# Moving the second projection piece of an element from step 2 to step 3 in a two-layer attention kernel

## The chip, the cores and the metric

The kernel runs on one core of a Trainium2 chip. The metric is device time in microseconds (us): the median of three runs before the change is 3305.34 us (3304.78 to 3305.59). Everything is computed in fp32, and the whole batch is one launch.

## What is computed

The input is `x` of shape (8, 512, 32, 32): 8 batch elements, 512 channels, 1024 positions. Two layers follow each other. Cut to what matters:

```python
# layer 0: group norm, 8-head attention (64 channels a head), projection, group norm, residual
hn  = group_norm(x, gn1_scale, gn1_bias)
qkv = einsum('bchw,oc->bohw', hn, w_qkv) + b_qkv
wgt = softmax(einsum('bct,bcs->bts', q * scale, k * scale))      # per head, 1024 x 1024
a   = einsum('bts,bcs->bct', wgt, v)
x   = x + group_norm(einsum('bchw,oc->bohw', a, w_proj) + b_proj, gn2_scale, gn2_bias)
# layer 1: weight-normed projections, one 512-channel head, output projection, residual
qkv = einsum('oc,bcn->bon', weight_norm(v_qkv), x);  qkv = qkv / rms(qkv)
h   = einsum('bij,bcj->bci', softmax(q.T @ k * C**-0.5), v)
out = (x + einsum('oc,bcn->bon', weight_norm(v_out), h)) * 2**-0.5
```

## The kernel before, in words

A loop (`for b in range(B)`, L1015) goes over the 8 elements. In each, layer 0's attention runs as 32 **steps** (`STEPS`, L335; the loop of L1018): step i handles one block of 128 query positions of one pair of heads, with 8 blocks to a pair (`j, r = divmod(i, NB)`, L1019). After the steps come the last values, the output projection and norm of layer 0, and all of layer 1, except that most of layer 1's last products are carried into the first steps of the next element: `fills` and `laters` (L1124 and L1125) put `one.products(1, c)` and `one.keep(1, c)`, for c of 1, 2 and 3, into steps 0, 1 and 2 of element b + 1. Step 3 gets empty lists.

Nothing is reordered by a scheduler: `InOrder` (L26) pins the instructions of every engine to the order in which the program states them. So the order of the work around the change is that of `Heads.step` (L490):

- `softmax(i)` (L432): for each of two heads a VectorE maximum over the 128x1024 scores in PSUM, then a ScalarE exp from PSUM into the tile `p`, with its row sums.
- `values`, on steps 5, 7, 9 and so on: the attention values of two earlier steps, 32 matmul instructions into a bank `po`.
- `fill`: what the caller hands in for TensorE. Here that is, in this order, a carried product of layer 1 and one **piece** of projections.
- `scores(i + 1)` (L417): four matmul calls (eight instructions in the profile) into two tiles `s` of 128x1024. These tiles come from `ps_s`, which has three buffers (L101). The order of the calls is first half of head 0, first half of head 1, second halves.
- `turn()` (L444): VectorE transposes the `p` of the step before, and four DMAs on SP's queue write it to `pT`.
- `scale()` (L462): a VectorE reciprocal, then two GpSimd (POOL) multiplications on `p`.
- `later`: a carried `keep` (two VectorE operations and, for the second half of the positions, an output DMA on SP's queue), then the piece's GpSimd addition, then, on steps 1, 3, 5 and 7 of elements 1 to 6, one GpSimd group-norm application `norm1.apply` (L1037).

A **piece** is one `yield` of `project_rows` (L363). For the next pair of heads it makes half of k or half of q. Eight matmul calls (16 instructions) use only 64 of the 128 rows each and alternate between two banks of `ps_m`; that pool has two buffers in all (L102), which the carried products and the values use too. ScalarE then empties both banks (L394 and L395), one into `qk` and one into a spare part of the tile `v`, and a GpSimd addition (L396) sums them. The four pieces of pair j + 1 must be done when step 8j + 7 issues the first scores of that pair. One piece is taken from `todo` on each step on which `(i - LAG) % RG` is not 0. With `LAG` 5 and `RG` 2 these are the even steps; the odd ones from 5 on have values.

For elements 1 to 7 TensorE's order at the start is therefore:

```
step 0: po(c=1)  piece 0  s(1)
step 1: po(c=2)           s(2)
step 2: po(c=3)  piece 1  s(3)
step 3:                   s(4)
step 4:          piece 2  s(5)
step 5: values            s(6)
step 6:          piece 3  s(7)
```

Here po(c) is the carried product of layer 1 (eight calls, 16 instructions), and s(n) the scores of step n. The scores of step 0 are issued ahead of the loop. In element 0 there is no carried product; steps 0 to 3 have one part each of that element's own values projection (L1012).

Of the kernel before, what the change touches and what calls it, by code (L numbers as in the profile page):

```python
# [52 lines left out]
def attention_blocks_kernel(  # L53
# [52 lines left out]
    def big(name, lead=CI):  # L106

        return slots.take([P, lead, CI * N // lead], name)
# [41 lines left out]
    def load_x(b, xt, ci):  # L150
        SY.dma_start(out=xt[:, ci, :], in_=xv[b, :, ci, :])
# [181 lines left out]
    RG, TG = 2, 2 * P  # L333
    NB = N // P
    STEPS, LAG = CI * NB, 5  # L335
    halves = (slice(0, D), slice(D, P))

    def project_qk(b, j, hn):

        qk = pair.tile([P, 2, N], F32, tag="qk", name=f"qk_{b}_{j}")  # L340
        kp = qk[:, 1, :].rearrange("p (be m) -> p be m", be=4)

        def pieces():
            for t in (1, 0):
                w = near["qk"][:, t]
                for th in range(2):
                    hs = slice(th * HN, (th + 1) * HN)
                    pm = bank(f"pqk_{b}_{j}_{t}_{th}")
                    run(matmuls(pm, [(w[:, ci, j * P : (j + 1) * P], hn[:, ci, hs]) for ci in range(CI)]))
                    if t == 0:  # L350
                        AC.activation(qk[:, 0, hs], pm, AF.Identity, bias=bqs[:, j : j + 1], scale=QSCALE0)
                    else:
                        AC.activation(
                            kp[:, :, th * P : (th + 1) * P],
                            pm.rearrange("p (m be) -> p be m", be=4),
                            AF.Identity,
                            bias=col(BK, j),
                        )
                    yield

        return qk, pieces()

    def project_rows(b, j, hn):  # L363

        qk = pair.tile([P, 2, N], F32, tag="qk", name=f"qk_{b}_{j}")
        kp = qk[:, 1, :].rearrange("p (be m) -> p be m", be=4)
        spare = near["v#"]

        def pieces():
            for t in (1, 0):
                w = near["qk"][:, t]
                scale = 1.0 if t else QSCALE0
                bias = col(BK, j) if t else bqs[:, j : j + 1]
                for th in range(2):
                    hs = slice(th * HN, (th + 1) * HN)
                    pms = [bank(f"pqk_{b}_{j}_{t}_{th}_{r}") for r in range(2)]
                    for ci in range(CI):
                        for r in range(2):  # L380
                            PE.matmul(
                                pms[r],
                                w[halves[r], ci, j * P : (j + 1) * P],
                                hn[halves[r], ci, hs],
                                start=(ci == 0),
                                stop=(ci == CI - 1),
                            )
                    to, rest = qk[:, 0, hs], spare[:, hs]
                    if t:

                        to = kp[:, :, th * P : (th + 1) * P]
                        rest = rest.rearrange("p (be m) -> p be m", be=4)
                        pms = [pm.rearrange("p (m be) -> p be m", be=4) for pm in pms]
                    AC.activation(to, pms[0], AF.Identity, bias=bias, scale=scale)  # L394
                    AC.activation(rest, pms[1], AF.Copy, scale=scale)  # L395
                    yield lambda to=to, rest=rest: PO.tensor_add(to, to, rest)  # L396

        return qk, pieces()
# [112 lines left out]
    def project_out_half(b, h, o):  # L511

        for j in range(CI):
            for th in range(2):
                pm = bank(f"ph_{b}_{j}_{th}")
                run(matmuls(pm, out_terms(h.a, j, th, range(CI // 2))))
                AC.activation(o[:, j, th * HN : (th + 1) * HN], pm, AF.Identity, bias=col(BP, j))
            yield
# [482 lines left out]
    qk0, todo = project_qk(0, 0, x0)  # L1001
# [13 lines left out]
    for b in range(B):  # L1015
        hn, more = heads.hn, b + 1 < B
        todo = iter(())
        for i in range(STEPS):  # L1018
            j, r = divmod(i, NB)  # L1019
            due = []  # L1020
            fill = [lambda: due.append(next(todo, None))] if (i - LAG) % RG else []
            early, later = [], []
            if i < CI:
                fill, later = fills[i] + fill, laters[i]
            if r == 0:
                if j + 1 < CI:
                    heads.qk[j + 1], todo = project_rows(b, j + 1, hn)
                elif more:
                    qk_next, todo = project_rows(b + 1, 0, hn_next)
                if j + 1 == CI:  # L1030
                    slots.give(f"hn_{b}")
                    if not more:
                        o_last = big(f"o_{b}")
                        todo = project_out_half(b, heads, o_last)
            later.append(lambda: [f() for f in due if f])

            if b and more and i % 2 and i < 2 * CI:  # L1037
                later.append(lambda: norm1.apply(i // 2, PO))
            if not b:


                if i == CI:
                    hn_next = big(f"hn_{b + 1}")
                    norm1 = Norm1(b + 1, hn_next)
                if 0 <= i - CI < CI:
                    later.append(lambda: load_x(b + 1, hn_next, i - CI))
                if 0 <= i - CI - 2 < 2 * CI:
                    later.append(lambda: norm1.stats((i - CI - 2) // 2, i % 2))
                k = i - 3 * CI - 2
                if k == 0:  # L1050
                    coeffs = norm1.gn.all_steps()
                    early += [norm1.aggregate, lambda: next(coeffs)]
                elif 0 < k < 8:
                    early.append(lambda: next(coeffs, None))
                if 0 <= k - 7 < CI // 2:
                    for ci in range(2):
                        later.append(lambda ci=ci: norm1.apply(2 * (k - 7) + ci, PO))

            if i == STEPS - NB + 1:
                xt = big(f"x_{b}")  # L1060
            if 0 <= i - (STEPS - NB + 1) < CI:
                later.append(lambda: load_x(b, xt, i - (STEPS - NB + 1)))
            heads.step(i, fill, early, later)
# [105 lines left out]
```

## Time and profile before

The profiled execution took 3305.39 us, of which its span is 3303.4 us and 1.99 us lie around it. It stands 0.05 us above the median of the runs.

| what | value |
|---|---|
| median of 3 runs | 3305.34 us |
| profiled execution, and its span | 3305.39 us, 3303.4 us |
| granted TensorE clock, mean | 0.998 |
| VectorE (DVE) busy | 2123.7 us, 64% |
| ScalarE (ACT) busy | 1073.0 us, 32% |
| GpSimd (POOL) busy | 982.8 us, 30% |
| DMA, mean | 124 GB/s |

All instructions carry the line of the pinning helper, L34, so groups are told apart by their tiles: `s` scores, `pqk` projection pieces, `po` values or carried products, `nm` the maxima, `p` the probabilities. In the chain of waits, each row is a start, a length and what ran; a TensorE row there runs from the start of its first instruction to the start of what follows. In the timeline a matmul's length is longer, as its modelled end is shown and matmuls overlap.

### The profile page before, as it was taken

How to read it: one execution, taken by the hardware profiler on the slowest of the kernel's cores; microseconds unless marked ns; L12 is line 12 of the kernel's file. 1: busy time of each engine (PE TensorE's matmuls, PEld its weight loads, DVE VectorE, ACT ScalarE, POOL GpSimd, SP SyncE). 2: the span in 40 equal slices, each digit the busy share in tenths (PEclk: the TensorE clock that was granted, in tenths of full speed). 3: DMA queues.
4: the chain of work that ended last, by engine and by line, in shares of the span. 5: the costliest groups of instructions: out<-in, count | busy, mean ns of one | idle time of the engine just before them, and what ended most of it. 6: DMA issues, size and time to landing. Idle time of an engine off the chain costs nothing.

```text
span 3303.4 us, 35653 instructions
## 1 busy us (share of the span) xinstructions
PE 3261.8 (99%) x13178; PEld 1603.1 (49%) x13178; DVE 2123.7 (64%) x2869; ACT 1073.0 (32%) x1813; POOL 982.8 (30%) x857
## 2 busy tenths in 40 slices
PE   8999999999999999999999999999999999999899
PEld 4444544445444454444544445444454445444354
DVE  4696647855478655885458754686646866468653
ACT  2453114521145211551215412254122531235210
POOL 0352124511255012550215403253023531235111
PEclk9999999999999999999999999999999999999999
DMA  5575205741168411782127811277213762057600
GB/s 188 187 201 166 79 34 149 203 152 67 38 167 213 134 45 51 184 223 95 45 77 190 231 55 59 84 197 213 77 39 103 198 181 89 13 133 199 185 7 26
DMA packets 182708, 410.82 MB, mean 124 GB/s; under 512 B 27621, under 2 KB 27657, under 8 KB 176521
## 3 DMA queue, kind: packets, MB, share of 16 engines
q1 hardware_dynamic: 182416, 408.53, 43.7%
q8 instruction: 105, 1.72, 0.2%
q14 instruction: 67, 0.54, 0.0%
q10 hardware_dynamic: 120, 0.02, 0.0%
HBM read 112.48 MB, written 27.56 MB: 42 GB/s over the span
## 4 chain that ended last, share of the span: by engine, by line
PE 98%; DVE 1%; DMA 0%; issue 0%; ACT 0%; SPq 0%; ACTq 0%; DVEq 0%
PE po L34 27%; PE s L34 14%; PE pqk L34 14%; PE pv L34 7%; PE p_e_T L34 7%; PE p_e_B L34 5%; PE py L34 4%; PE p_u_T L34 3%; PE p_v_T L34 3%; PE p_o_T L34 3%; PE p_v_B L34 3%; PE p_u_B L34 2%; PE p_o_B L34 2%; PE pG L34 1%; PE pA L34 0%; PE pB L34 0%
## 5 line engine op out<-in xcount | busy, mean ns | idle before, releaser
L34 POOL TENSOR_SCALAR p<-p,tt 128x1024 f32<-128x1024 f32 x512 | 566.0, 1118 | 926.7 <-DVE tt L34 926.7
L34 ACT ACTIVATE p<-s,nm 128x1024 f32<-128x1024 f32 x512 | 565.5, 1109 | 848.7 <-DVE nm L34 799.3
L34 DVE TENSOR_REDUCE nm<-s 128x1 f32<-128x1024 f32 x512 | 602.7, 1219 | 224.5 <-PE s L34 224.3
L34 DVE STREAM_TRANSPOSE pb<-p 128x2048 f32<-128x2048 f32 x256 | 589.6, 2303 | 24.7 <-POOL p L34 19.3
L34 PE MATMUL s<-qk 64*128 64x512 f32 x2048 | 515.0, 603 | 12.4 <-ACT p L34 12.4
L34 PE MATMUL pqk<-hn,qk 64*128 64x512 f32 (+1 forms) x2016 | 479.9, 591 | 0.0
L34 PE MATMUL po<-pT,v 128*64 128x256 f32 x4096 | 470.3, 382 | 3.4 <-DMA pT<-pb 3.2
L34 PE MATMUL po<-e,v 128*128 128x512 f32 x1024 | 451.7, 595 | 0.0
L34 PEld LDWEIGHTS po<-pT,v 128*64 128x64 f32 x4096 | 284.1, 137 | 226.8 <-ACT v L34 79.6
L34 PEld LDWEIGHTS pqk<-hn,qk 64*128 64x128 f32 (+1 forms) x2016 | 204.3, 187 | 252.2 <-issue 243.0
L34 PEld LDWEIGHTS s<-qk 64*128 64x128 f32 x2048 | 196.1, 186 | 252.8 <-issue 232.9
L34 PEld LDWEIGHTS po<-e,v 128*128 128x128 f32 x1024 | 191.9, 190 | 245.0 <-issue 236.4
L34 POOL TENSOR_TENSOR u<-u,xy 128x512 f32<-128x512 f32 x64 | 79.0, 1272 | 770.7 <-DMA xy<-far_rinv 671.4
L34 PE MATMUL pv<-v,hn 128*128 128x512 f32 x512 | 229.0, 598 | 0.0
L34 DVE TENSOR_TENSOR e<-e,p_e_T 128x512 f32<-128x512 f32 x160 | 107.0, 685 | 145.1 <-PE p_e_T L34 142.9
L34 POOL TENSOR_TENSOR qk<-qk,v 128x512 f32<-128x512 f32 x124 | 158.2, 1276 | 83.9 <-ACT v L34 83.9
L34 ACT ACTIVATE e<-e,shift,rinv 128x512 f32<-128x512 f32 x128 | 100.9, 812 | 247.7 <-DVE e L34 247.7
L34 POOL TENSOR_TENSOR esum<-esum,e 128x512 f32<-128x512 f32 x96 | 121.5, 1267 | 163.9 <-ACT e L34 161.4
L34 PEld LDWEIGHTS pv<-v,hn 128*128 128x128 f32 x512 | 94.6, 190 | 115.1 <-issue 114.8
L34 PE MATMUL p_e_T<-s,t 128*128 128x512 f32 x320 | 147.8, 592 | 0.0
L34 PE MATMUL py<-x,gram 128*128 128x512 f32 x320 | 141.5, 602 | 6.0 <-issue 6.0
L34 ACT COPY v<-pv 128x1024 f32<-128x1024 f32 x32 | 32.2, 1007 | 259.4 <-PE pv L34 243.7
(186 smaller groups left out, 3068.3 us busy)
## 6 DMA issues: line engine op xcount, KB each, us to landing
pT<-pb SPq DMA_DIRECT2D x1024, 256.0 KB, 4.2
hn<-in_x_dram SPq DMA_DIRECT2D x32, 512.0 KB, 5.4
x<-in_x_dram SPq DMA_DIRECT2D x32, 512.0 KB, 5.6
out_dram<-x SPq DMA_DIRECT2D x32, 512.0 KB, 2.6
score<-far_score SPq DMA_DIRECT2D x8, 1792.0 KB, 7.5
value<-far_value SPq DMA_DIRECT2D x8, 1792.0 KB, 7.0
qk<-far_qk SPq DMA_DIRECT2D x7, 2048.0 KB, 7.9
proj<-far_proj SPq DMA_DIRECT2D x7, 1792.0 KB, 10.4
```

The source lines that it names most:

```text
L34: return lambda *args, **kw: self._pin(call(*args, **kw))
```

## The change

For elements 1 to 7, step 2 no longer takes a piece and step 3 takes one. All other steps, and element 0, are as before. A piece that is taken brings along its matmuls, its two ScalarE evictions and, in `later`, its GpSimd addition. Pieces then fall on steps 0, 3, 4 and 6 of the first pair of heads.

```diff
         for i in range(STEPS):
             j, r = divmod(i, NB)
             due = []
-            fill = [lambda: due.append(next(todo, None))] if (i - LAG) % RG else []
+
+            projects = (i - LAG) % RG if not b or i not in (2, 3) else i == 3
+            fill = [lambda: due.append(next(todo, None))] if projects else []
             early, later = [], []
             if i < CI:
                 fill, later = fills[i] + fill, laters[i]
```

TensorE's order at the start of elements 1 to 7 becomes:

```
step 0: po(c=1)  piece 0  s(1)
step 1: po(c=2)           s(2)
step 2: po(c=3)           s(3)
step 3:          piece 1  s(4)
step 4:          piece 2  s(5)
step 5: values            s(6)
step 6:          piece 3  s(7)
```

## The prediction

> **What bounds the kernel now.** I read the page first, its busy times and its chain.
>
> ```profile
> PE 3261.8 (99%) x13178; PEld 1603.1 (49%) x13178; DVE 2123.7 (64%) x2869; ACT 1073.0 (32%) x1813; POOL 982.8 (30%) x857
> ...
> PE 98%; DVE 1%; DMA 0%; issue 0%; ACT 0%; SPq 0%; ACTq 0%; DVEq 0%
> ```
>
> TensorE (PE) is busy nearly throughout, and 98% of the chain that ended last is PE. So a microsecond counts only if it comes off PE's own line. DVE's 1% is the hint: there are a few places where PE waits for the softmax. The waits, for PE alone, say where:
>
> ```profile
> PE s L34 <- ACT p L34: 12.4, 7, 1.8
> PE py L34 <- issue: 6.0, 1, 6.0
> ```
>
> The largest wait, twice the next, falls 7 times, and there are 7 elements with a step 3 that has only scores. The 1.8 us is counted from a modelled matmul end, so I take the size from the chain around step 3 of element 1, which begins where po(c=3) of step 2 has been issued:
>
> ```profile
> 526.23 4.05 PE pqk L34 x15
> ...
> 530.71 0.89 PE s L34 x5
> 531.60 0.02 issue
> 531.62 1.24 DVE nm L34
> ...
> 532.94 1.21 ACT p L34 x2
> ...
> 534.20 1.55 PE s L34 x5
> ...
> 536.18 3.00 PE pqk L34 x14
> ...
> 539.61 1.72 PE s L34 x7
> ```
>
> Read it as: piece 1 and s(3) up to 531.60; then nothing new on PE until 534.20, as s(4)'s second matmul needs the buffer that holds head 0 of s(3), which is free only after its maximum (1.24 us) and exp (1.21 us) have read it. The gap is 534.20 - 531.60 = **2.60 us**. The values of step 5 begin at 539.61 + 1.72 = 541.33. From 526.23 that makes **15.10 us**. The same stretch in the six other elements is 926.36 to 941.46, 1327.48 to 1342.59, 1727.62 to 1742.72, 2127.75 to 2142.85, 2527.89 to 2542.99 and 2927.57 to 2942.67: 15.10 or 15.11 each.
>
> The next steps show the same loop with a piece or values between two scores, and no gap:
>
> ```profile
> 541.33 3.60 PE po L34 x32
> 544.93 1.92 PE s L34 x8
> 546.85 3.43 PE pqk L34 x16
> 550.28 1.72 PE s L34 x8
> ```
>
> These rows are my prices: scores after a product cost 1.92, a piece after scores 3.43, scores after a piece 1.72.
>
> **What the Trainium skill says.** "Perfetto Trace Analysis", Optimization Strategy: the same gap recurring on the engine that should be saturated can mean that buffers of SBUF or PSUM ran out. The trace agrees: seven equal gaps, each a wait for one of the three `s` buffers. "PSUM — Partial Sum Buffer", Engine vs sequencer instructions: matmuls start and complete in program order. So a blocked score also blocks the piece behind it, though that piece needs nothing from it; here piece 2 starts at 536.18, right behind the late s(4). "TensorE: Matmul & The Clock Gate", Part 3, The mechanism: a weight load overlaps matmuls in flight only where the row group differs. The trace agrees in this: 16 instructions of 589 ns (median) in a piece take 3.43 us, 0.43 us a pair, so two row halves run at once.
>
> **The change part by part.** I re-lay the stretch from 526.23, the issue end of po(c=3), where PE's order is unchanged so far.
>
> Removed: piece 1 ahead of s(3), 15.10 us of old stretch in all. Its parts are piece 1 and s(3), 531.60 - 526.23 = 5.37; the gap, 2.60; s(4), 536.18 - 534.20 = 1.98; piece 2, 3.43; s(5), 1.72. Sum 15.10.
>
> In its place: s(3) after a product 1.92, piece 1 after scores 3.43, s(4) 1.72, piece 2 3.43, s(5) 1.72. Sum **12.22 us**, if no new wait comes in. The difference is 2.88: the gap's 2.60, and 0.28 since s(3) with piece 1 falls from 5.37 to 5.35 and s(4), whose halves now run beside others again, from 1.98 to 1.72.
>
> Whether waits come in I check engine by engine; times are element 1's. The timeline of step 6 is the template, as it has scores that end at 546.85, a piece, and scores:
>
> ```profile
> 548.20 1.11 ACT L34 ACTIVATE p<-s,nm 128x1024 f32<-128x1024 f32 x1 [2.75 <-DVE nm L34]
> ...
> 550.39 0.69 ACT L34 ACTIVATE qk<-pqk,bqs 128x512 f32<-128x512 f32 x1
> 550.96 0.60 ACT L34 ACTIVATE v<-pqk 128x512 f32<-128x512 f32 x1
> ```
>
> *The old gap.* s(3) ends at 526.23 + 1.92 = 528.15. In the template the first exp is over 549.31 - 546.85 = 2.46 us after its scores: 530.61. s(4)'s blocked matmul is due at 528.15 + 3.43 = 531.58. The cover is 0.97 us; without it the chain would stick out by what is lacking.
>
> *The two banks.* One of piece 1's two banks last held po(c=3); `keep` reads it from 526.26 for 0.69 us, so it is free at 526.95, and piece 1 now asks at 528.15. Piece 2 follows with only s(4) between, which nothing in the trace before shows. The template's second eviction ends 551.56 - 546.85 = 4.71 us after the scores: 532.86; piece 2 starts at 528.15 + 3.43 + 1.72 = 533.30. The slack is 0.44 us. Cost from both sides: 0 if the template holds, 0.5 us if both evictions come one eviction (0.6 to 0.7 us) later and a little more of the slack goes; below nothing is excluded, as PE's rows are already its shortest. I take 0.
>
> *VectorE.* Its rows behind the gap show how fast it can go when it is behind:
>
> ```profile
> 531.62 2.36 DVE L34 TENSOR_REDUCE nm<-s 128x1 f32<-128x1024 f32 x2 [3.94 <-PE s L34]
> ...
> 536.16 2.33 DVE L34 TENSOR_REDUCE nm<-s 128x1 f32<-128x1024 f32 x2
> ...
> 540.87 2.33 DVE L34 TENSOR_REDUCE nm<-s 128x1 f32<-128x1024 f32 x2
> ```
>
> A step takes 4.54 and 4.71 us there, against PE's new 3.43 + 1.72 = 5.15. `keep` of step 2 ends at 527.68, before s(3) does. So reduces start with their scores at 528.18, 533.33 and 538.48, with transposes and reciprocals between; the exp of s(4) ends at 533.30 + 2.46 = 535.76, ahead of the 536.73 at which s(5) needs its buffer. Cost 0.
>
> *GpSimd.* The piece's addition (1.26 us) moves into step 3, behind the two multiplications (2.21) and ahead of `norm1.apply` (1.19):
>
> ```profile
> 536.34 2.21 POOL L34 TENSOR_SCALAR p<-p,tt 128x1024 f32<-128x1024 f32 x2 [3.65 <-DVE tt L34]
> 538.54 1.19 POOL L34 TENSOR_SCALAR hn<-hn,a,c 128x1024 f32<-128x1024 f32 x1
> ```
>
> Step 3's sum is 4.66 of 5.15 us. In times: from 533.0, after the reciprocal, the queue is done at 537.7. Step 4's multiplications follow its reciprocal, which stands behind the maxima (533.33 to 535.69) and step 3's transpose (2.30, to 538.0): they are due at 538.2. They wait for nothing new. The first reader of the sum is the scores of the next pair in step 7.
>
> *ScalarE and SP.* The evictions (0.69 and 0.60 us) move behind step 3's exps and ahead of step 4's, due at 534.65, and end at 532.86. The piece issues no DMA. The transpose of step 2's `p` ends near 532.8 in place of 536.19, so its four DMAs go out 3.4 us sooner; the slot they write was given up by po(c=3) or by the output DMA issued at 527.71, whose kind lands in 2.6 us (median), so no wait. `pT` is read in steps 5 and 7 and later.
>
> Sum: 7 x 2.88 = 20.16 us. Element 0 has nothing. Against the profiled execution's own time of 3305.39 us, which is the median plus 0.05, that is **3285.2 us**. Behind step 5 everything follows PE, so the rest is shifted, not changed.
>
> **The rivals.**
>
> 1. *A part comes back at piece 2*: evictions later than the template, or exps held by VectorE at s(5). For it: the bank slack is only 0.44 us, and two pieces with one set of scores between are new. Against it: all offsets come from rows that recur. At 0.5 us an element 3288.7; at 1 us 3292.2.
> 2. *The softmax takes over*: the same wait reappears a step later and half the gap returns. The time is 3305.4 - 10.1 = 3295.3. Against it stand VectorE's 4.54 and 4.71 us a step.
> 3. *GpSimd makes it slower*: in step 3 three jobs queue up; if they run longer than their rows (the page calls POOL spans rough), step 4's multiplications are late, then the transpose of its `p`, then the maxima of s(6), then s(7). To reach PE, the queue must use up 0.5 us before the multiplications, 0.45 before the transpose (due at 538.48 + 2.36 = 540.84), 0.8 before the maxima (543.2 against the end of s(6) at 538.45 + 3.60 + 1.92 = 543.97) and 0.97 of cover: 2.7 us. It must then lose the 2.88 won; from 5.6 us of lateness an element on, the change is a loss, and at 6.6 us the time is 3305.4 + 7 = 3312.4. Nothing in the rows points there.
> 4. *It does nothing*: the piece is taken from the same generator, and pieces on steps 0, 3, 4 and 6 are all in time for step 7. Only if the gap belonged to something else than the `s` buffers would the time stay at 3305; the chain names the exp.
>
> **How the numbers follow.** Forecast, 3283 to 3288: 0.78. Rival 1, to 3293: 0.13. Rival 2: 0.04. Rival 3: 0.03, of which nearly all ends slower. Rival 4: 0.02. About 0.2%, 6.6 us, is what a measurement here can tell from no change. Faster by more, below 3298.7, is the forecast with rivals 1 and 2: 0.95; within, 0.02; slower, 0.03. The range takes the forecast's own, and of rival 1 what lies below 0.7 us an element (3290.1): 3283 to 3290. The low end is the forecast less 0.3 us an element, in case neighbouring rows overlap more than priced.
>
> **What would show it.** Right: the wait of `s` for the exp is gone from PE's list; the chain from po(c=3) to the values of step 5 has PE rows alone and is 12.2 us long in each of seven elements; a piece of 3.43 stands between s(3) and s(4). Wrong: a PE row that waits for `v` or `qk` evictions (rival 1), for `p` again at s(5) or s(6) (rival 2), or the POOL multiplications of step 4 starting later than their reciprocal (rival 3).

## The result, and the profile after

The changed kernel takes **3284.2 us** (median of 4 runs, 3283.51 to 3284.92) against 3305.06 us (4 runs, 3303.73 to 3305.59). The ratio is 0.9938, 95% interval 0.9920 to 0.9955: 20.9 us faster, where 20.16 was forecast. The profiled execution took 3283.51 us, 21.9 us less than that of before.

The page's busy times and the engines' shares in its chain, of the changed kernel:

```profile
PE 3251.9 (99%) x13178; PEld 1602.3 (49%) x13178; DVE 2124.0 (65%) x2869; ACT 1072.3 (33%) x1813; POOL 982.7 (30%) x857
...
PE 96%; DVE 1%; DMA 1%; SPq 1%; issue 1%; POOL 0%; ACTq 0%; DVEq 0%
```

PE is busy 9.9 us **less**, with the same 13178 matmuls. A gap that closes leaves busy time alone, so something besides the gap has gone. That is taken up below.

The waits of PE, of the changed kernel (total, times, longest):

```profile
PE py L34 <- issue: 6.0, 1, 6.0
PE pG L34 <- DVE w_qk L34: 5.5, 1, 5.5
...
PE po L34 <- DMA pT<-pb: 3.6, 2, 2.9
```

The line of `s` waiting for `p`, 12.4 us in 7 waits, is gone, and nothing has come in its place. PE's waits for `pT` are 3.6 us where they were 3.2; that the chain now has 1% of DMA means only that in the last element it runs back through the writes of `pT` in place of PE's rows.

The chain from po(c=3) to the values of step 5, element 1, of the changed kernel:

```profile
518.38 7.06 PE po L34 x16
525.44 1.92 PE s L34 x8
527.36 3.43 PE pqk L34 x16
530.79 1.72 PE s L34 x8
532.51 3.43 PE pqk L34 x16
535.94 1.72 PE s L34 x8
537.66 3.60 PE po L34 x32
```

Five rows of PE alone, 537.66 - 525.44 = **12.22 us**, each with the length that was priced. Between the profiles the start of those values comes sooner by 2.88 to 2.89 us more in each further element, apart from element 3. The 21.9 us are 7 x 2.88 = 20.2, and two differences that the edit doesn't make: 0.8 us in the opening, where the `pG` matmuls took 28.33 us against 29.17 while the first loads came in (DMA share 0.99 and 0.97), and 1.0 us late in element 2 of the profile before. There one transpose waited for a write of `pT`:

```profile
1074.37 2.31 DVE L34 STREAM_TRANSPOSE pb<-p 128x2048 f32<-128x2048 f32 x1 [2.47 <-DMA pT<-pb]
```

The scores that followed took 2.71 us in place of 1.72. These 1.8 us are about the spread of the runs. In the medians the change gained 20.9 us here and 21.0 in a repeat on another chip (below), 0.7 to 0.8 more than 20.2; what makes that up is not shown.

What the other engines do in steps 3 and 4, of the changed kernel:

```profile
531.47 0.60 ACT L34 ACTIVATE v<-pqk 128x512 f32<-128x512 f32 x1
```

```profile
532.10 2.21 POOL L34 TENSOR_SCALAR p<-p,tt 128x1024 f32<-128x1024 f32 x2 [6.77 <-DVE tt L34]
534.28 1.27 POOL L34 TENSOR_TENSOR qk<-qk,v 128x512 f32<-128x512 f32 x1
535.54 1.19 POOL L34 TENSOR_SCALAR hn<-hn,a,c 128x1024 f32<-128x1024 f32 x1
537.25 2.21 POOL L34 TENSOR_SCALAR p<-p,tt 128x1024 f32<-128x1024 f32 x2 [0.52 <-DVE tt L34]
```

The second eviction ends at 532.07 and piece 2 starts at 532.51: the slack of 0.44 us is there as worked out. POOL does its four jobs and is then idle for 0.52 us before step 4's multiplications, where 0.5 was given.

### The profile page after: what moved, and what is told of

The parts are those of the page before. It is cut to its first block, busy times and chain, and to the rows that moved or that the text cites. A ratio compares the mean times of both kernels' runs of the same rounds, so it can differ in the third digit from the quotient of the medians.

```text
span 3281.5 us, 35660 instructions
## 1 busy us (share of the span) xinstructions
PE 3251.9 (99%) x13178; PEld 1602.3 (49%) x13178; DVE 2124.0 (65%) x2869; ACT 1072.3 (33%) x1813; POOL 982.7 (30%) x857
## 3 DMA queue, kind: packets, MB, share of 16 engines
q8 instruction: 105, 1.72, 0.2%
## 4 chain that ended last, share of the span: by engine, by line
PE 96%; DVE 1%; DMA 1%; SPq 1%; issue 1%; POOL 0%; ACTq 0%; DVEq 0%
PE po L34 27%; PE s L34 13%; PE pqk L34 13%; PE pv L34 7%; PE p_e_T L34 7%; PE p_e_B L34 5%; PE py L34 4%; PE p_u_T L34 3%; PE p_v_T L34 3%; PE p_o_T L34 3%; PE p_v_B L34 3%; PE p_u_B L34 3%; PE p_o_B L34 2%; DMA pT<-pb 1%; PE pG L34 1%; DVE pb L34 1%
## 5 line engine op out<-in xcount | busy, mean ns | idle before, releaser
L34 DVE STREAM_TRANSPOSE pb<-p 128x2048 f32<-128x2048 f32 x256 | 589.3, 2302 | 20.9 <-POOL p L34 18.7
L34 PE MATMUL s<-qk 64*128 64x512 f32 x2048 | 502.2, 602 | 0.0
L34 PE MATMUL pqk<-hn,qk 64*128 64x512 f32 (+1 forms) x2016 | 467.3, 590 | 0.0
```

What stands on the lines that cost most here:

```text
L34: return lambda *args, **kw: self._pin(call(*args, **kw))
```

## The experiments

All ratios are to the kernel before, run on the same chip.

**Work in the gap.** To before:

```diff
+            if b and i == 3:
+                fill = [lambda: idle_piece(b, hn)]
...
+    def idle_piece(b, hn):
+        w = near["qk"][:, 1]
+        pms = [bank(f"idle_{b}_{r}") for r in range(2)]
+        for ci in range(CI):
+            for r in range(2):
+                PE.matmul(
+                    pms[r], w[halves[r], ci, P : 2 * P], hn[halves[r], ci, HN:], start=(ci == 0), stop=(ci == CI - 1)
+                )
```

> Order of before, with piece 1 in step 2, and in step 3 of elements 1 to 7 a second run of piece 1's 16 matmul instructions into two banks that nothing reads (the output is unchanged by it). Theory (TensorE idles 2.60 us in step 3 for want of an s buffer, so any work there is hidden): the stretch from po(c=3) to the values of step 5 is 5.37 + 3.43 + 1.72 + 3.43 + 1.72 = 15.67 us against 15.10, so 24 us of added matmuls cost 7 x 0.57 = 4 us: about 3309, and the wait of s for the exp is gone. Rival (the gain came from taking the piece out of step 2, where it shares banks and queues with the carried product): the added work is paid in full, 3305 + 7 x 3.43 = 3329.

Measured: 3314.27 against 3304.0, ratio 1.0033 (1.0020 to 1.0046). The chain of this kernel from po(c=3) on (`idle` is the tile of the added work):

```profile
524.83 4.05 PE pqk L34 x15
...
528.89 0.42 PE pqk L34
529.32 1.29 PE s L34 x6
...
531.03 3.00 PE idle L34 x14
...
541.33 3.60 PE po L34 x32
```

The wait for the exp is gone, and the added work is neither paid in full nor as cheap as I had said: the stretch is 541.33 - 524.83 = 16.50 us, 1.40 more than before (7 x 1.40 = 9.8; measured 10.3). So of 3.43 us the gap hid 3.43 - 1.40 = **2.03**, and not 2.86. My 5.37 us for piece 1 with s(3) is the term that misled: the chain of before leaves PE at 531.60 for the maximum that releases it, which is when head 0's scores of s(3) were done, not when all of s(3) was issued.

Step 0 of the kernel before has the same piece and scores behind a product and no gap, so it gives the true price. Its chain:

```profile
503.98 4.05 PE pqk L34 x15
...
508.04 0.42 PE pqk L34
508.46 1.72 PE s L34 x7
510.18 1.91 PE po L34 x4
```

That is 510.18 - 503.98 = 6.20 us, where scores first and then the piece take 1.92 + 3.43 = 5.35. The old stretch is therefore 6.20 + **2.03** + 1.72 + 3.43 + 1.72 = 15.10, and the gain per element 2.88 = 2.03 (gap) + **0.85** (the piece no longer stands right behind a product). Of the 2.03, 1.77 is idle time, as the list of waits had it (12.4 / 7), and 0.26 is the blocked s(4), 1.98 for 1.72. Why the place costs 0.85 shows in the list of waits around the kernel before's piece 1:

```profile
PEld pqk L34 <- DVE v L34: 0.6, 1, 0.6
```

The piece's second bank is the one from which `keep` reads po(c=3), from 526.26 for 0.69 us. In that time PE, which works in order, does only the first matmul call of the piece; the weights for the second bank follow at 527.01. No run takes away this wait alone, so 0.85 as its price rests on the two sums above and on the traces.

**Half a piece in the gap.** To before; step 3 takes from `todo` too:

```diff
+            projects = (i - LAG) % RG or (b and i == 3)
+            fill = [lambda: due.append(next(todo, None))] if projects else []
...
                     for ci in range(CI):
+                        if ci == 2 and b and (j, t, th) == (1, 1, 1):
+                            yield None
```

> Piece 1 is split: its first eight matmul instructions stay in step 2, the other eight, with evictions and addition, stand in step 3. Theory (a fixed delay of 2.60 us from s(3) to s(4), covered as far as the work in between reaches): half a piece covers 1.72 of 2.60, a gap of 0.88 stays, the stretch is 13.4 us, the gain 1.7 an element: 3305 - 12 = 3293. Rival (the piece must be out of step 2 altogether, as po(c=3) and keep hold its bank): the first half still waits there, so little is gained: 3303 to 3305.

Measured: 3295.11, ratio 0.9972 (0.9961 to 0.9983), 8.9 us faster than before. The stretch is 539.62 - 525.79 = 13.83 us, 1.27 less than before (7 x 1.27 = 8.9). The half piece hides its own 1.72 us in the gap, all of it, and 0.45 are lost again, since piece 2 with its scores takes 5.60 and not 5.15. The weight loads (PEld) in that stretch show both that wait, for the evictions of piece 1, and what the rival named, the first half of piece 1 waiting for `keep`:

```profile
PEld pqk L34 <- DVE v L34: 0.6, 1, 0.6
PEld pqk L34 <- ACT qk L34: 0.5, 1, 0.5
PEld pqk L34 <- ACT v L34: 0.2, 1, 0.2
```

So the cover counts by its length up to 2.03, and the 0.85 of the place behind a product is still paid.

**Evictions and addition alone.** To before; step 3 takes from `todo` too:

```diff
+            projects = (i - LAG) % RG or (b and i == 3)
+            fill = [lambda: due.append(next(todo, None))] if projects else []
...
+                    if b and (j, t, th) == (1, 1, 1):
+                        yield None
                     to, rest = qk[:, 0, hs], spare[:, hs]
```

> Only the two ScalarE evictions and the GpSimd addition of piece 1 move to step 3; its matmuls stay in step 2. Theory: TensorE's order is that of before, s(4) waits for the exp as before, stretch 15.10, time 3305. Rival (ScalarE's evictions ahead of step 3's exps, or the addition in step 2, held up the exp that s(4) waits for): most of the gain comes, 3285 to 3290.

Measured: 3308.99, ratio 1.0016 (1.0009 to 1.0022): nothing gained. The 7 waits of `s` for `p` are there as before:

```profile
PE s L34 <- ACT p L34: 12.4, 7, 1.8
```

Element 1's stretch is 541.49 - 525.94 = 15.55, 0.45 longer, once more because piece 2 waits for a bank that is emptied late. That is 3.2 of the 5.0 us lost; in elements 5 and 7 of its profile the granted clock fell as well (last section). The rival, that ScalarE's or GpSimd's part of the move makes the gain, is out.

**Another product in the gap.** To before:

```diff
             fills = [[lambda c=c: one.products(1, c)] for c in range(1, CI)]
             laters = [[lambda c=c: one.keep(1, c)] for c in range(1, CI)]
+            fills.insert(2, [])
+            laters.insert(2, [])
+            fills[3].append(lambda b=b: [slots.give(f"v1_{b}"), slots.give(f"e_{b}_1")])
...
-                for name in (f"v1_{b}", f"e_{b}_1", f"x_{b}"):
+                for name in (f"x_{b}",):
...
-            laters[CI - 2].append(done)
+            laters[CI - 1].append(done)
```

> The pieces stay on steps 0, 2, 4 and 6, and the carried product po(c=3) with its keep moves from step 2 to step 3 instead (two slots of the older element are given up right behind its matmuls). Theory (any product between s(3) and s(4) that lasts over 2.6 us closes the gap): from the end of po(c=2), s 1.92, piece 3.43, s 1.72, po 7.06, s 1.92, piece 3.43, s 1.72 = 21.2 us, the same sum as in the changed kernel, time 3284 to 3286. Rival (the piece itself has to leave step 2): 3305.

Measured: 3284.84, ratio 0.9941 (0.9926 to 0.9956), like the changed kernel. From the end of po(c=2) to the values of step 5 it takes 538.41 - 517.21 = 21.20 us, the sum expected. It is not this piece that has to move: with a whole product between s(3) and s(4), and no piece right behind a product in step 2, the gain is the same.

**The gap moved on.** To before:

```diff
+            projects = (i - LAG) % RG if not b or i not in (3, 4) else i == 3
```

> Piece 1 stays in step 2 and piece 2 moves from step 4 to step 3, so step 4 is left with scores alone. Theory (any step without a product shows the gap): the gap goes from s(4) to s(5), stretch again about 15.1 us, time 3304 to 3306. Rival (something particular to step 3, such as the end of the carried work, makes the wait): a piece in step 3 is enough and the time is 3285.

Measured: 3308.22, ratio 1.0010 (1.0004 to 1.0017). The 7 waits for `p` stand at s(5), and the stretch is 540.88 - 525.78 = 15.10 us. So the gap goes with the step that has no product, here as in step 3, and the rival is out. The 3.8 us that were not expected lie behind the gap: in elements 2, 4 and 6 of its profile the granted clock fell. Stretches of this kernel, first the values of step 5 in elements 4 and 3, then three pieces of the time right behind the gap in element 4 (start and end, length, busy times of PE, PEld, DVE, ACT and POOL with their instructions, clock, DMA share, GB/s):

```profile
1743.33:1748.15 4.82, 4.82 (x34) 2.73 (x34) 4.25 (x4) 2.30 (x4) 2.33 (x3) 0.75 0.86 241
1342.78:1346.38 3.60, 3.60 (x34) 2.21 (x34) 3.51 (x5) 2.30 (x4) 2.21 (x2) 1.00 0.83 215
...
1742.00:1742.35 0.35, 0.35 (x4) 0.08 (x1) 0.35 (x1) 0.00 (x0) 0.35 (x1) 1.00 0.69 152
1742.37:1745.77 3.40, 3.40 (x14) 1.48 (x14) 3.31 (x5) 1.58 (x3) 2.38 (x3) 0.50 0.83 204
1745.79:1746.10 0.31, 0.31 (x6) 0.20 (x4) 0.31 (x1) 0.31 (x1) 0.00 (x0) 1.00 0.95 350
```

The same 32 instructions take 4.82 us at a mean clock of 0.75 and 3.60 at 1.00. The mean mixes two values: for 3.4 us the clock is 0.50, and it is full on both sides. The scores ahead of the values fall into it too. From po(c=3) to the end of the values, the elements with a dip take 20.34 us and those without one 18.70, so a dip costs 1.64 us, and three of them 4.9; the profiled execution is 4.75 above the median of before.

**ScalarE's slack.** To the changed kernel:

```diff
-                    AC.activation(to, pms[0], AF.Identity, bias=bias, scale=scale)
-                    AC.activation(rest, pms[1], AF.Copy, scale=scale)
+                    for _ in range(2 if b and (j, t, th) == (1, 1, 1) else 1):
+                        AC.activation(to, pms[0], AF.Identity, bias=bias, scale=scale)
+                        AC.activation(rest, pms[1], AF.Copy, scale=scale)
```

> The changed kernel, with both ScalarE evictions of piece 1 done twice (the same values). The evictions end 1.29 us later, where the changed kernel's trace has 0.44 us between their end (532.07) and the start of piece 2 (532.51). Theory of the prediction (this slack is all there is ahead of piece 2): piece 2 waits 0.85 to 0.95 us, the stretch is 13.1 us, time 3284 + 6 = 3290. Rival (the banks have no part in it, other queues give way): 3284.

Measured: 3291.65, ratio 0.9962 (0.9947 to 0.9977). The stretch is 538.63 - 525.47 = 13.16 us, 0.94 over the changed kernel's (7 x 0.94 = 6.6). A new line stands in PE's list:

```profile
PE pqk L34 <- ACT qk L34: 1.4, 7, 0.2
```

So the 0.44 us were real and were all there was. The list shows only 0.2 us a time, as the first bank's wait; the rest is the second bank's, during which PE counts as busy with the first call.

**GpSimd's slack.** To the changed kernel, with n of 2 and of 4:

```diff
             later.append(lambda: [f() for f in due if f])
+            if b and i == 3:
+                sh = near["v#"][:, N : N + HN]
+                later.append(lambda: [PO.tensor_add(sh, sh, sh) for _ in range(n)])
```

> The changed kernel with two more GpSimd additions of 1.27 us (on an unused part of v) behind the piece's addition in step 3, 2.54 us in all. The prediction said GpSimd may be late by 2.7 us in step 3 before TensorE waits. Theory: no change, 3284 to 3286. Rival (the slack on GpSimd is only the 0.5 us to its next work): 2 us an element, 3298.

> The same with four more additions, 5.08 us. Theory: 5.08 - 2.7 = 2.4 us late at TensorE in elements 1 to 7, 3284 + 17 = 3301. Rival of full payment behind 0.5 us: 3316. If GpSimd's lateness is taken up before it gets to TensorE: 3284.

Measured: 3283.69, ratio 0.9939 (0.9922 to 0.9955), with two, and 3294.94, ratio 0.9972 (0.9961 to 0.9982), with four. Two change nothing. With four, POOL and then PE of element 1 show:

```profile
534.96 4.39 POOL L34 TENSOR_TENSOR v<-v 128x512 f32<-128x512 f32 x4
```

```profile
547.59 1.98 PE L34 MATMUL s<-qk 64*128 64x512 f32 x6 [0.68 <-ACT p L34]
```

The four took 4.39 us, not the 5.08 that I had multiplied out. From po(c=3)'s end to the end of s(7) it is 549.57 - 524.89 = 24.68 us, against 548.33 - 525.44 = 22.89 in the changed kernel: 1.79 lost. So the queue could be 4.39 - 1.79 = 2.60 us late before PE felt it; the prediction had 2.7 and had named s(7). Six waits are listed; element 7, without `norm1.apply`, has more room. 6 x 1.79 = 10.7 us; the run with four is 11.3 above the one with two.

**The same TensorE order, another ScalarE order.** To before, with `behind` run in `step` right after the scores:

```diff
+            behind = []
+            if b and i == 2:
+                behind, fill = fill, []
...
                 self.scores(i + 1)
+            for f in behind:
+                f()
```

> TensorE's order of the changed kernel (po(c=3), s(3), piece 1, s(4), piece 2), but piece 1 is issued in step 2, behind s(3), so ScalarE's queue has its two evictions ahead of step 3's exps and not behind them. Theory: the exp of s(3) then waits until the piece is done and emptied (3.43 + 0.64 = 4.1 us behind s(3)) and ends at 5.2, s(4)'s second matmul is due at 3.43, so TensorE waits 1.5 to 1.8 us again: stretch near 14.0 of 15.10, time 3297. Rival (only TensorE's order matters): 3284.

Measured: 3304.99, ratio 1.0002 (0.9994 to 1.0011): no gain. ScalarE in element 1 of this kernel:

```profile
532.02 0.69 ACT L34 ACTIVATE qk<-pqk,cols 128x512 f32<-128x512 f32 x1 [8.79 <-PE pqk L34]
532.61 0.59 ACT L34 ACTIVATE v<-pqk 128x512 f32<-128x512 f32 x1
533.08 1.12 ACT L34 ACTIVATE p<-s,nm 128x1024 f32<-128x1024 f32 x1
```

The evictions wait for the piece, and the exp that s(4) needs waits behind them. In element 2, where the clock stayed full, the stretch is 14.8 us by the timeline. That is 0.8 over my estimate, as the eviction starts when the whole piece is done and I had it sooner; the gain left is 7 x 0.3 = 2 us. The profiled execution, the highest of 12 at 3312.03, shows dips of the clock in elements 1, 3 and 7, as the kernel with the gap at s(5) did, and there the stretch is 16.5 us. Such dips would hide a gain of 2 us; that they did so in the other runs is not shown.

**The same for piece 0.** To the changed kernel, with `b and i == 0`, and the changed kernel beside it:

> The changed kernel, and in step 0 of elements 1 to 7 piece 0 stands behind s(1) in place of between po(c=1) and s(1). Theory (a piece right behind a carried product costs 4.05 + 0.43 us in place of 3.43, as its second bank waits for keep to read the product; with s(1) it makes 6.20 against 1.92 + 3.43 = 5.35): 0.85 us an element less, 3284.2 - 6 = 3278, if the first eviction frees a bank for po(c=2) in time; half of it, 3281, if po(c=2) waits for that eviction. Rival (all of the gain of the change was the wait for the s buffer): no change, 3284.

> The changed kernel once more, on the chip of the two others, to compare them with: 3284.

Measured: 3283.66 (ratio 0.9938, 0.9924 to 0.9951) and, for the changed kernel, 3283.22 (0.9937, 0.9925 to 0.9950): the same. The chain of the first, behind po(c=1):

```profile
503.23 1.92 PE s L34 x8
505.15 3.48 PE pqk L34 x16
508.63 0.68 ACT qk L34
...
509.36 7.13 PE po L34 x16
```

The piece does take its short 3.48 us. But po(c=2) now waits 0.7 us for the first eviction, so 6.13 us stand for 6.20. This fits the reading that the place behind a product costs 0.85 us because two banks change hands with nothing in between; here the same handover happens on the other side of the piece. The time is the rival's, the mechanism is the theory's worse case and worse than I gave it. No version that beats the changed kernel came out of this.

## Why the prediction was right, point by point

- *The bound and the place.* Right. PE sets the time, the seven gaps are those of one missing product, and what PE gained the end gained: element by element 2.88 us, in the sum 20.2.
- *The new stretch.* Right in each term: 12.22 us with rows of 1.92, 3.43, 1.72, 3.43 and 1.72.
- *The split of the 2.88.* Wrong. "The gap's 2.60, and 0.28" was to be 2.03 of gap (with the blocked s(4)) and 0.85 from the piece leaving its place behind po(c=3). The failed step is "piece 1 and s(3), 531.60 - 526.23 = 5.37". The chain's row for s(3) stops at the scores that released the maximum, and I took that for the end of s(3) and of PE's work ("nothing new on PE until 534.20"). The rest of s(3) and the first call of s(4) ran on until 532.43, where the 1.77 us of idle time begin. In the same way piece 2 starts at 535.17, beside the last of s(4), and not at 536.18, where only the chain's row begins. The sum was untouched, as it compares two whole stretches, but the price of added work was off (4 us forecast, 10.3 measured). I had also set aside the 1.8 us of the list of waits, which was the true idle time, and PE's 9.9 us of lower busy time are the trace of the other part: 7 x (0.85 + 0.26) = 7.8, and the 1.8 us of opening and late write, 9.6 together.
- *The banks.* Right. The slack of 0.44 us is in the trace and was used up by doubled evictions to within 0.1 us.
- *VectorE.* Right: its maxima start within 0.1 us of the ends of their scores in steps 3 to 6, and no PE wait leads to it.
- *GpSimd.* Right: 0.5 us of room at once, 2.6 (2.7 given) before PE waits.
- *ScalarE and SP.* Right for this edit. That the evictions come behind step 3's exps was named but not priced. The run that put them ahead shows what hangs on it: 14.8 us in an element with a full clock, 2.6 of the 2.88 lost.
- *The rivals.* None occurred. Rivals 1 and 3 could be brought about, each at the point that had been worked out.

Open: why the clock dips behind some gaps and not behind others. It did so in three kernels of the experiments and not in the profile of before, with gaps of like length. The last section has what the traces show of it.

## What to carry to other kernels

A step without work for the bounding engine can lay bare the chain that its neighbours hide, so put something there that lasts longer than the chain, and check that the work's own epilogue sits behind, not ahead of, the instructions which the next step waits for. Compare whole stretches between two points that the edit doesn't touch: sums of rows cut at a jump of the chain gave me the right total with the wrong parts. When an engine's busy time falls with the same instructions, look for a wait that was hidden inside it; with two buffers, look for handovers with nothing in between.

## What the runs showed of the hardware

Behind a gap of PE in steps 3 or 4, with 1.5 to 1.8 us of idle time, the granted clock fell in some elements: in three of seven with the gap at s(5), in two of seven where only the evictions and the addition moved, in three with piece 1 behind s(3). Neither the kernel before, with the same gap, nor the changed one shows it there. Each dip is at 0.50, lasts 3.41 us, begins 0.3 to 1.7 us behind the gap and costs 1.5 to 1.7 us.

The dips do not come at any time. In each of the 13 traces all changes of the granted clock lie whole multiples of 3.413 us apart, and each of these dips is one such step. With the gap at s(5) the dips of elements 2, 4 and 6 are 802.13 us apart, 235 steps, so an element takes about half a step more than a whole number, and the gap falls at other places of the step in even and in odd elements. Counted in steps from these changes, it begins at 0.06 to 0.13 of a step in the three with a dip, and at 0.64 to 0.91 in the four others. Place alone is not the rule, though: in the kernel before the gaps begin at 0.00 to 0.78 of a step and none brings a dip.

The runs with the gap at s(5) also spread more: 3303.8 to 3310.3 us over 20 runs, against 3282.6 to 3284.9 over nine of the changed one. GpSimd's additions with one operand tile for both inputs and output took 1.08 to 1.10 us each (2.16 for two, 4.39 for four), where additions of two tiles of that size take 1.27.
